# An attention and feed-forward block on one core: a re-ordered start, with the first pair's weight columns split first

## The chip, the core and the metric

The kernel runs on one core of a Trainium2 chip. A core has a matrix engine (TensorE, PE in the profile, with its weight loads shown as PEld), a vector engine (DVE), a scalar engine (ACT), a general engine (GpSimd, POOL) and a queue engine (SP) that starts most transfers. The engines run their own instruction streams in order and wait for one another through semaphores. The metric is the time of one execution on the device in microseconds (us).

## What is computed

The input x has 8 batches of 512 rows of 256 numbers. Cut to what matters, the reference is:

```python
x = x + attention(layernorm(x))    # rms_norm with gamma, w_qkv (256 x 3072), 16 heads of 64, softmax, w_out
x = x + ffn(layernorm(x))          # gelu(x @ w1 + b1) @ w2 + b2, scaled by the sum of the top-2 router weights
```

Everything is in 32-bit floating point. The first normalisation is a layernorm followed by an rms norm whose gamma is folded into w_qkv; attention is `softmax(q k^T / 8) v` for 8 x 16 heads.

## The kernel before, in words

**Arithmetic.** Every product is made from 16-bit operands in three parts. An operand is split into a high part (the value scaled and rounded to 16 bits, written by ACT) and a low part (what the rounding lost, written by DVE with a `SCALAR_TENSOR_TENSOR`, or on POOL for the softmax numerators). The three products are high x high, low x high and high x low (`PARTS`). The scale is a power of two, found on the chip from a sum of squares: `square` (ACT) squares a weight block and sums along the row, `total` adds over the 128 partitions with a product with ones on PE into the PSUM tile `pn`, and `powers` works out the exponent with seven tiny DVE instructions. `with_gamma` multiplies the factor by `gam1` = 1 + gamma, on DVE. `find_qk` does this for half of the q and k columns (512 each, four pairs of heads); its second part `rest()` (seven more tiny DVE instructions) finds the output scale `ab` that the eviction of q and k needs. `find_v` does it for v.

**The start.** `load_x(0)`, gamma and the blocks q0, k0, v0, v1 of w_qkv are loaded at once, into the four buffers of the pool `stage`; q1 and k1 (columns 512 to 1023) and the inputs of batches 1 to 3 stand behind them on SP, and q1 and k1 wait for buffers of `stage`. PE meanwhile runs `WARM` = 80 products of zeros into a bank of the pool `ps_m`. DVE finds mean and variance of batch 0 (`sums1`), `scale1` turns them into factors (two POOL instructions with the operation pow), `normalize` writes the normalised rows, and `transpose_rows` turns them with PE into the tile `pt` and splits them into `xnT`. `part_qk` splits the q0 and k0 blocks 512 columns at a time into `wqk`, and `project_qk(0, n)` makes q and k of the first pair of heads; its `high` is an ACT instruction into `QT` or `KT`, its `low` a DVE instruction.

**The loop.** The attention part has 128 steps. A step takes two tiles of scores: `scores` on PE into the two double buffers of `ps_s`, `top` (the row maximum, DVE, tile `mx`), `exp` (four ACT instructions into `e`), `high` (ACT casts e into `hl`), `low` (four POOL subtractions) and a transposing transfer on SP into `hT` (7 buffers). Three steps later `weigh` multiplies by V and `divide` (DVE) divides. A pair of heads of one batch has four tiles of scores, so it takes two steps. Everything else is hung on the steps by hand: `at(step, pos, fn, ...)` puts a piece of work at a place of a step. Within a step the order of issue is: the scores and their maxima, the low parts left over, `"d"`, the products of `"a"`, the exponentials, `"e"`, the evictions of `"a"` (high parts on ACT, then low parts on DVE), the casts of e, `weigh` and `divide`, `"b"`, `"z"`. `at` adds one to the step of every `"d"`. `Core.keep_order` keeps this order on all engines. So ACT and DVE, on which maxima, exponentials and all high and low parts lie, serve a step's items strictly in the written order.

In the first steps hang `split_wv` (w_v), `make_v` (V of batch 0), `project_qk` of the next pairs, the squares of q1 and k1 (`squares("qk1", ...)`, ACT, step 2), `find_qk` for them (step 3), `split_qk1` (steps 4 and 5), and for batch 1 `sums1` (step 1), `scale1` (steps 1 to 3), `normalize` (POOL, steps 3 and 4) and `transpose_rows` (steps 6 and 8).

After the attention steps comes the feed-forward part (`expand`, `contract`), which the change does not touch.

Of the kernel before, what the change touches and what calls it, by code (L numbers as in the profile page):

```python
# [11 lines left out]
F32 = mybir.dt.float32  # L12
F32R = mybir.dt.float32r
F16 = mybir.dt.float16
BF16 = mybir.dt.bfloat16
# [11 lines left out]
P = 128  # L27
LAG = 6
RING = 2
VW = 130  # L30
WARM = 80
EARLY = 6
# [44 lines left out]
def preln_block(  # L77
# [61 lines left out]
    for name, off, eng in (  # L139
        ("q0", 0, nc.scalar), ("k0", INNER, nc.sync), ("v0", 2 * INNER, nc.sync),  # L140
        ("v1", 2 * INNER + 512, nc.sync), ("q1", 512, nc.sync), ("k1", INNER + 512, nc.sync),
    ):
        raw[name] = staged(f"w_{name}", wqkv_r[:, :, off : off + 512], eng)
    for b in range(1, XB):
        load_x(b)
    w_r = const.tile([P, NC, NE], F32, name="w_r")
# [23 lines left out]

    def split(hi, lo, src, f):

        nc.scalar.activation(hi, src, AF.Copy, scale=f)
        return lambda: nc.vector.scalar_tensor_tensor(lo, src, f, hi, ALU.mult, ALU.subtract)
# [4 lines left out]
    def square(name, col, src, scale=1.0):  # L179

        pool, what = (hl_p, "hT") if name in ("qk0", "v") else (stage, "stage")
        junk = pool.tile([P, 1024], BF16, tag=what, name="junk", bufs=HTB if what == "hT" else SB)
        nc.scalar.activation(
            junk[:, 0 : src.shape[-1]], src, AF.Square, scale=scale,
            accum_out=sums[name][:, col[0], col[1] : col[1] + 1],
        )

    def square_v(name, col, src):
        junk = stage.tile([P, 512], BF16, tag="stage", name="junk")
        nc.vector.scalar_tensor_tensor(  # L190
            junk, src, 1.0, src, ALU.mult, ALU.mult,
            accum_out=sums[name][:, col[0], col[1] : col[1] + 1],
        )
# [41 lines left out]

    def with_gamma(name, s):

        f = stat.tile([P, 2, NC], F32, name=f"f_{name}")
        for i in range(2):
            nc.vector.tensor_scalar(f[:, i, :], gam1, s[:, i : i + 1], None, ALU.mult)  # L240
        return f

    def find_qk(half, n2):

        v = nc.vector
        added(n2)
        s, u, z = powers(f"qk{half}", n2)
        factors["qk", half] = with_gamma(f"qk{half}", s)  # L250

        def rest():
            ab = stat.tile([P, 2], U32, name=f"ab_{half}")
            w = stat.tile([P, 1], U32, name=f"w_{half}")
            v.tensor_copy(w, u[:, 1:2])
            v.tensor_tensor(z[:, 0:1], u[:, 0:1], w, ALU.add)
            v.tensor_scalar(z[:, 0:1], z[:, 0:1], 101, 254, ALU.add, ALU.min)
            v.tensor_scalar(w, z[:, 0:1], 1, None, ALU.logical_shift_right)
            v.tensor_tensor(u[:, 0:1], z[:, 0:1], w, ALU.subtract)
            v.tensor_scalar(ab[:, 0:1], u[:, 0:1], 23, None, ALU.logical_shift_left)  # L260
            v.tensor_scalar(ab[:, 1:2], w, 23, None, ALU.logical_shift_left)
            factors["out", half] = ab.bitcast(F32)

        return rest

    def find_v(n2):
        added(n2)
        s, u, z = powers("v", n2)
        factors["v"] = with_gamma("v", s)
        factors["1/v"] = inverses("v", u, z)  # L270
# [29 lines left out]
    with ExitStack() as att:  # L300
# [13 lines left out]
        VT = [work.tile([P, HEADS, VW], F16, tag=f"VT{r}", name=f"VT{r}") for r in range(NT)]  # L314

        wv = [work.tile([P, NC, INNER], F16, name=f"wv{i}") for i in range(2)]
        wo = [work.tile([P, NP, D], F16, name=f"wo{i}") for i in range(2)]
# [11 lines left out]

        def part_qk(n, half, c):  # L330
            i = "qk".index(n)
            hi, lo = (w[:, c, i, ts(half, 512)] for w in wqk)
            return split(hi, lo, raw[f"{n}{half}"][:, c], factors["qk", half][:, i, c : c + 1])

        def squares(name, i, key):
            for c in range(NC):
                square(name, (i, c), raw[key][:, c, :], gam1[:, c : c + 1])

# [9 lines left out]
        def split_qk1(n, c):  # L348
            part_qk(n, 1, c)()
            done("wqk")  # L350

        def split_wv(c, j):
            cols = ts(j, 512)
            f = factors["v"][:, j, c : c + 1]
            split(wv[0][:, c, cols], wv[1][:, c, cols], raw[f"v{j}"][:, c, :], f)()
            done("wv", j)
# [36 lines left out]

        def scale1(b, part):


            g = nc.vector if b == 0 else nc.gpsimd
            mv = norm1[b][0]
            if part == 0:
                rstd = tiny.tile([P, NT], F32, tag="rstd", name="rstd")  # L400
                g.tensor_scalar(rstd, mv[:, :, 1], LN_EPS, None, ALU.add)
                nc.gpsimd.tensor_tensor(rstd, rstd, halves[:, 0, :], ALU.pow)
                nm = tiny.tile([P, NT], F32, tag="nm1", name="nm1")
                g.tensor_scalar(nm, mv[:, :, 0], -1.0, None, ALU.mult)
                norm1[b] += [nm, rstd]
                return
            norm = tiny.tile([P, NT], F32, tag="norm", name="norm")
            g.tensor_scalar(norm, mv[:, :, 1], float(D), 1e-30, ALU.mult, ALU.max)
            nc.gpsimd.tensor_tensor(norm, norm, halves[:, 1, :], ALU.pow)
            _, nm, rstd = norm1[b]  # L410
            g.tensor_tensor(norm, norm, rstd, ALU.mult)
            g.tensor_scalar(norm, norm, NORM_EPS, float(D) ** -0.5, ALU.max, ALU.mult)
            norm1[b] = [nm, None, norm, rstd]
# [11 lines left out]
        def normalize(norm, b, t, tag):  # L425
# [5 lines left out]
            c = slice(t, t + 1)  # L431
            eng = nc.vector if (tag, b) == ("x", 0) else nc.gpsimd
            src = (xs if tag == "x" else x2)[b]
# [4 lines left out]
        def transpose_rows(b, c):  # L438

            if c == 0:  # L440
                xnT[b] = work.tile([P, NC, 2, S], F16, tag="xnT", bufs=2, name=f"xnT{b}")
            pt = bank("pt")
            need(NT, "xn", "x", b)
# [58 lines left out]
        def project_qk(pair, n):  # L502

            b, p = divmod(pair, NP)
            need(NC, "xnT", b)
            if p >= NP // 2:
                need(2 * NC, "wqk")
            pm = bank("pqk")
# [220 lines left out]

        warm = bank("warm")  # L730
        for i in range(WARM):
            nc.tensor.matmul(warm[:, 0:256], cold[:, 0:P], cold, start=True, stop=True)

# [5 lines left out]
        nc.vector.tensor_scalar_add(gam1, gam, 1.0)  # L739
        scale1(0, 0)  # L740
        scale1(0, 1)
        for name, k, m in (("qk0", 2, NC), ("v", 2, NC), ("qk1", 2, NC), ("o", 3, 1), ("w", 3, 4)):
            new_sums(name, k, m)
        for i in range(2):
            squares("qk0", i, "qk"[i] + "0")
        scale1_rest(0)
        scale1_last(0)
        for t in range(NT):
            normalize(norm1, 0, t, "x")
        squares("v", 0, "v0")  # L750
        rest = find_qk(0, total("qk0"))
        parts = [transpose_rows(0, c) for c in range(NC)]
        lows = [part_qk("q", 0, c) for c in range(NC)]
        for high, _ in parts:
            high()
        lows += [part_qk("k", 0, c) for c in range(NC)]
        for _, low in parts:
            low()
        for low in lows:
            low()  # L760
        rest()
        squares("v", 1, "v1")
        for high, low in [project_qk(0, n) for n in range(2)]:
            high()
            low()
        lows = [find(find_v, "v")[1]]


# [42 lines left out]

        for c in range(NC):
            at(0, "e", split_wv, c, 0)
            at(1, "e", split_wv, c, 1)
            at(4, "e", split_qk1, "q", c)
            at(5, "e", split_qk1, "k", c)
        for i in range(2):
            at(1, "d", squares, "qk1", i, "qk"[i] + "1")
        at(3, "b", find_rest, find_qk, 1, "qk1")
# [20 lines left out]
        for b in range(B):  # L840
# [10 lines left out]
            if b + 1 < B:  # L851
                at(max(s0 - 5, 1), "d", scale1_rest, b + 1)
                at(s0 - 4 if b else 2, "d", scale1_last, b + 1)
                for t in range(NT):
                    at(s0 + 21 + 2 * t, "a", project, b, 1, t)
                    at(max(s0 - 9 + t // 2, 0), "d", sums1, b + 1, t)
                    at(s0 + (1 + t if b else 2 + t // 2), "d", normalize, norm1, b + 1, t, "x")
                at(max(s0 - 7, 0), "d", scale1, b + 1, 0)
                at(max(s0 - 6, 0), "d", scale1, b + 1, 1)
                if b + XB < B:  # L860
                    for t in range(NT):
                        at(s0 + 30 + 2 * t, "d", load_x_piece, b + XB, t)
                for c in range(NC):
                    at(s0 + 6 + 2 * c, "b", transpose_rows, b + 1, c)
        del units[-2, "a"]
# [210 lines left out]
```

## Time and profile before

| what | us |
|---|---|
| median of 3 runs (971.69 to 971.80) | 971.78 |
| the profiled execution, its own time | 971.25 |
| its span, first to last instruction | 969.4 |
| PE busy in the span | 940.3 (97%) |
| ACT busy | 844.3 (87%) |
| DVE busy | 729.3 (75%) |
| POOL busy | 692.8 (71%) |
| mean granted TensorE clock | 0.996 |

A busy share is the time in which an engine's recorded instructions run. The granted clock is the share of full speed at which TensorE was let run. In the listings a row reads: start, length, engine, line (nearly always L48, the helper through which all instructions are issued, so tiles are what tells rows apart), operation, output tile, input tiles, shape, count, and in brackets how long the engine had stood idle and what released it.

### The profile page before, as it was taken

The numbers are of one execution on the slowest core, as the hardware profiler recorded it, in microseconds if no ns is written. First come the engines' busy times: TensorE is split into PE (matmuls) and PEld (weight loads), VectorE is DVE, ScalarE is ACT, GpSimd is POOL, SyncE is SP. The second block draws the span as 40 slices with busy tenths as digits, with TensorE's granted clock in tenths as the row PEclk, the third lists the DMA queues.
The fourth block names the chain that finished last, engine by engine and source line by source line (L and its number), as shares of the span: only waits on it lengthen the run. The fifth ranks groups of instructions, "written<-read, shape, count | busy, mean of one in ns | idle before, by whom it ended". The sixth has DMA issues, their size and how long they took to land.

```text
span 969.4 us, 27965 instructions
## 1 busy us (share of the span) xinstructions
PE 940.3 (97%) x11290; PEld 603.3 (62%) x11290; DVE 729.3 (75%) x1314; ACT 844.3 (87%) x1267; POOL 692.8 (71%) x713
## 2 busy tenths in 40 slices
PE   7788999999999999999999999999999999999998
PEld 5345566666666666666666666666666666666666
DVE  5878878988788878888877887777877865665554
ACT  5989899999999999999999999899999986767772
POOL 1677879788888888888888787877798963543400
PEclk9999999999999999999999999999999999999999
DMA  5598889999999999999989989889899991233111
GB/s 165 140 203 170 161 194 202 228 201 195 201 197 198 202 205 200 201 202 214 186 191 192 197 166 194 185 177 175 179 187 187 204 163 31 73 71 88 49 45 39
DMA packets 570193, 161.36 MB, mean 166 GB/s; under 512 B 552528, under 2 KB 568016, under 8 KB 570064
## 3 DMA queue, kind: packets, MB, share of 16 engines
q1 hardware_dynamic: 569520, 158.78, 80.3%
q8 instruction: 89, 1.46, 0.6%
q10 hardware_dynamic: 544, 0.79, 0.2%
q14 instruction: 40, 0.33, 0.1%
HBM read 14.82 MB, written 6.29 MB: 22 GB/s over the span
## 4 chain that ended last, share of the span: by engine, by line
PE 59%; DVE 18%; ACT 16%; issue 4%; POOL 2%; ACTq 0%; POOLq 0%
ACT e L48 11%; PE po L48 10%; PE ps L48 10%; PE pqk L48 9%; PE pf L48 9%; PE ph L48 8%; DVE mx L48 7%; PE pp L48 6%; PE pv L48 4%; DVE QT L48 2%; DVE KT L48 2%; DVE O L48 2%; DVE VT L48 2%; PE pot L48 2%; ACT QT L48 2%
## 5 line engine op out<-in xcount | busy, mean ns | idle before, releaser
L48 POOL TENSOR_TENSOR hl<-e,hl 128x512 f16<-128x512 f32 x512 | 583.5, 1171 | 139.8 <-issue 88.3
L48 ACT ACTIVATE e<-ps,mx 128x512 f32<-128x512 f32 x512 | 310.2, 690 | 52.2 <-DVE mx L48 44.6
L48 DVE TENSOR_REDUCE mx<-ps 128x2 f32<-128x1024 f32 x256 | 300.3, 1213 | 5.1 <-PE ps L48 5.0
L48 ACT CAST hl<-e 128x1024 f16<-128x1024 f32 x256 | 259.2, 1083 | 0.0
L48 PEld LDWEIGHTS <-hT 128*128 128x128 f16 x6144 | 203.5, 97 | 32.3 <-issue 4.4
L48 PE MATMUL po<-VT,hT 128*128 128x65 f16 (+1 forms) x6144 | 207.9, 193 | 1.4 <-DVE VT L48 0.8
L48 PE MATMUL ps<-KT,QT 64*128 64x512 f16 x1536 | 192.1, 380 | 11.8 <-ACT e L48 10.4
L48 PE MATMUL pqk<-xnT,wqk 128*128 128x512 f16 x768 | 178.8, 382 | 7.6 <-DVE VT L48 3.7
L48 PEld LDWEIGHTS <-wqk 128*128 128x128 f16 x768 | 70.3, 98 | 111.8 <-issue 33.2
L48 PEld LDWEIGHTS <-QT 64*128 64x128 f16 x1536 | 67.3, 94 | 90.4 <-issue 28.1
L48 DVE SCALAR_TENSOR_TENSOR QT<-pqk,ab,QT 128x512 f16<-128x512 f32 x64 | 48.0, 750 | 77.6 <-ACT QT L48 77.6
L48 DVE SCALAR_TENSOR_TENSOR h<-h,s_w,h 128x512 f16<-128x512 f32 x64 | 50.1, 784 | 62.9 <-ACT h L48 62.9
L48 PE MATMUL pp<-wo,OT 128*128 128x256 f16 x768 | 95.1, 273 | 0.1
L48 PE MATMUL pv<-wv,xnT 128*128 128x512 f16 x384 | 93.3, 379 | 1.8 <-DVE QT L48 1.6
L48 PEld LDWEIGHTS <-OT 128*128 128x128 f16 x768 | 70.2, 98 | 33.0 <-issue 11.8
L48 PE MATMUL ph<-yT,w1s 128*128 128x512 f16 x384 | 89.6, 379 | 0.1
L48 PE MATMUL pf<-w2s,h 128*128 128x256 f16 x768 | 88.4, 273 | 0.0
L48 ACT ACTIVATE h<-ph,b,si_w 128x512 f32<-128x512 f32 x64 | 49.3, 770 | 41.7 <-PE ph L48 41.5
L48 PEld LDWEIGHTS <-h 128*128 128x128 f16 x768 | 75.1, 98 | 14.5
L48 DVE TENSOR_TENSOR VT<-pv,VT 128x512 f16<-128x512 f32 x64 | 43.8, 689 | 52.5 <-ACT VT L48 52.5
L48 PEld LDWEIGHTS <-xnT 128*128 128x128 f16 x384 | 37.3, 98 | 37.0 <-issue 4.9
L48 PEld LDWEIGHTS <-w1s 128*128 128x128 f16 x384 | 37.0, 98 | 36.8 <-issue 0.3
(128 smaller groups left out, 856.4 us busy)
## 6 DMA issues: line engine op xcount, KB each, us to landing
hT<-hl SPq DMA_TRANSPOSE x256, 3.9
w<-in_L_ffn_w_dram SPq DMA_DIRECT2D x32, 128.0 KB, 2.7
out_dram<-res SPq DMA_DIRECT2D x32, 128.0 KB, 1.7
x<-x SPq DMA_DIRECT2D x16, 128.0 KB, 2.6
x<-in_L_attn_x_dram SPq DMA_DIRECT2D x16, 128.0 KB, 2.8
x2s<-x SPq DMA_DIRECT2D x4, 512.0 KB, 3.6
x<-in_L_attn_x_dram SPq DMA_DIRECT2D x3, 512.0 KB, 8.1
w_k<-in_L_attn_w_qkv_dram SPq DMA_DIRECT2D x2, 512.0 KB, 6.2
```

Source lines behind the costliest of these rows:

```text
L48: i = method(*args, **kw)
```

## The change

- The squares of v0 and of k1 move from ACT to DVE (`square_v` with the factor `gam2` = gam1 squared); those of q1 are issued earlier, before the loop and in step 0; those of k1 at the ends of steps 1 and 2.
- q0 and k0 are split in three pieces of columns: the first 128 (the first pair of heads), the next 128, and the last 256. The low parts of the first piece come before the rest; `rest()` stands between the low parts of q and those of k; the last piece's low parts and `find_v` come in step 0.
- `with_gamma` becomes two tiny ACT instructions.
- `scale1` uses one pow instruction on 8 columns in place of two on 4. Of batch 0's four `normalize` instructions two move to POOL.
- `WARM` becomes 54 products at the start, 12 after the first transposes and 8 after the first pair's projections. The warming products and the first transposes use the two buffers of `ps_s`, no longer banks of `ps_m`.
- q1 and k1 are loaded by four transfers into buffers of the tag `OT`, which are free at the start, so they and the inputs of batches 1 to 3 wait for nothing.
- `split_wv` of the second half moves from step 1 to steps 2 and 3; for batch 1 `sums1` moves to steps 2 and 3, `scale1` to step 4, `normalize` to steps 6 and 7, `transpose_rows` to steps 8 and 9.

```diff
 VW = 130
-WARM = 80
+WARM = 54, 12, 8
 EARLY = 6
...
         ("q0", 0, nc.scalar), ("k0", INNER, nc.sync), ("v0", 2 * INNER, nc.sync),
-        ("v1", 2 * INNER + 512, nc.sync), ("q1", 512, nc.sync), ("k1", INNER + 512, nc.sync),
+        ("v1", 2 * INNER + 512, nc.sync),
     ):
-        raw[name] = staged(f"w_{name}", wqkv_r[:, :, off : off + 512], eng)
-    for b in range(1, XB):
-        load_x(b)
+        t = staged(f"w_{name}", wqkv_r[:, :, off : off + 512], eng)
+        raw[name] = [t[:, c, :] for c in range(NC)]
     w_r = const.tile([P, NC, NE], F32, name="w_r")
...
-    def split(hi, lo, src, f):
-
-        nc.scalar.activation(hi, src, AF.Copy, scale=f)
+    def split(hi, lo, src, f, eng=nc.scalar):
+
+        if eng is nc.scalar:
+            eng.activation(hi, src, AF.Copy, scale=f)
+        else:
+            eng.tensor_scalar(hi, src, f, None, ALU.mult)
         return lambda: nc.vector.scalar_tensor_tensor(lo, src, f, hi, ALU.mult, ALU.subtract)
...
-        pool, what = (hl_p, "hT") if name in ("qk0", "v") else (stage, "stage")
+        pool, what = (hl_p, "hT") if name in ("qk0", "v", "qk1") else (stage, "stage")
         junk = pool.tile([P, 1024], BF16, tag=what, name="junk", bufs=HTB if what == "hT" else SB)
...
-    def square_v(name, col, src):
-        junk = stage.tile([P, 512], BF16, tag="stage", name="junk")
+    def square_v(name, col, src, scale=1.0):
+        pool, what, n = (hl_p, "hT", HTB) if name in ("v", "qk1") else (stage, "stage", SB)
+        junk = pool.tile([P, 512], BF16, tag=what, name="junk", bufs=n)
         nc.vector.scalar_tensor_tensor(
-            junk, src, 1.0, src, ALU.mult, ALU.mult,
+            junk, src, scale, src, ALU.mult, ALU.mult,
             accum_out=sums[name][:, col[0], col[1] : col[1] + 1],
...
-    def with_gamma(name, s):
-
-        f = stat.tile([P, 2, NC], F32, name=f"f_{name}")
+    powers_of = {}
+
+    def with_gamma(*key):
+
+        f = stat.tile([P, 2, NC], F32, name="f_" + "".join(map(str, key)))
+        s = powers_of[key if len(key) > 1 else key[0]]
+        factors[key if len(key) > 1 else key[0]] = f
         for i in range(2):
-            nc.vector.tensor_scalar(f[:, i, :], gam1, s[:, i : i + 1], None, ALU.mult)
-        return f
+            nc.scalar.activation(f[:, i, :], gam1, AF.Copy, scale=s[:, i : i + 1])
...
         s, u, z = powers(f"qk{half}", n2)
-        factors["qk", half] = with_gamma(f"qk{half}", s)
+        powers_of["qk", half] = s
...
         s, u, z = powers("v", n2)
-        factors["v"] = with_gamma("v", s)
+        powers_of["v"] = s
         factors["1/v"] = inverses("v", u, z)
...
+        for name, off in (("q1", 512), ("k1", INNER + 512)):
+            raw[name] = []
+            for c in range(NC):
+                t = work.tile([P, 512], F32, tag="OT", name=f"w_{name}", bufs=8)
+                nc.sync.dma_start(out=t, in_=wqkv_r[:, c, off : off + 512])
+                raw[name].append(t)
+        for b in range(1, XB):
+            load_x(b)
+
         wv = [work.tile([P, NC, INNER], F16, name=f"wv{i}") for i in range(2)]
...
-        def part_qk(n, half, c):
+        def part_qk(n, half, c, cols=slice(0, 512), eng=nc.scalar):
             i = "qk".index(n)
-            hi, lo = (w[:, c, i, ts(half, 512)] for w in wqk)
-            return split(hi, lo, raw[f"{n}{half}"][:, c], factors["qk", half][:, i, c : c + 1])
-
-        def squares(name, i, key):
-            for c in range(NC):
-                square(name, (i, c), raw[key][:, c, :], gam1[:, c : c + 1])
+            hi, lo = (w[:, c, i, ts(half, 512)][:, cols] for w in wqk)
+            src = raw[f"{n}{half}"][c][:, cols]
+            for p in range(cols.start // P, cols.stop // P):
+                done("wqk", NP // 2 * half + p)
+            return split(hi, lo, src, factors["qk", half][:, i, c : c + 1], eng)
+
+        def squares(name, i, key, chunks=range(NC)):
+            for c in chunks:
+                square(name, (i, c), raw[key][c], gam1[:, c : c + 1])
...
             part_qk(n, 1, c)()
-            done("wqk")
...
             f = factors["v"][:, j, c : c + 1]
-            split(wv[0][:, c, cols], wv[1][:, c, cols], raw[f"v{j}"][:, c, :], f)()
+            split(wv[0][:, c, cols], wv[1][:, c, cols], raw[f"v{j}"][c], f)()
             done("wv", j)
...
-        def scale1(b, part):
+        def scale1(b):
...
             mv = norm1[b][0]
-            if part == 0:
-                rstd = tiny.tile([P, NT], F32, tag="rstd", name="rstd")
-                g.tensor_scalar(rstd, mv[:, :, 1], LN_EPS, None, ALU.add)
-                nc.gpsimd.tensor_tensor(rstd, rstd, halves[:, 0, :], ALU.pow)
-                nm = tiny.tile([P, NT], F32, tag="nm1", name="nm1")
-                g.tensor_scalar(nm, mv[:, :, 0], -1.0, None, ALU.mult)
-                norm1[b] += [nm, rstd]
-                return
-            norm = tiny.tile([P, NT], F32, tag="norm", name="norm")
-            g.tensor_scalar(norm, mv[:, :, 1], float(D), 1e-30, ALU.mult, ALU.max)
-            nc.gpsimd.tensor_tensor(norm, norm, halves[:, 1, :], ALU.pow)
-            _, nm, rstd = norm1[b]
+            both_p = tiny.tile([P, 2, NT], F32, tag="norm", name="norm")
+            g.tensor_scalar(both_p[:, 0, :], mv[:, :, 1], LN_EPS, None, ALU.add)
+            g.tensor_scalar(both_p[:, 1, :], mv[:, :, 1], float(D), 1e-30, ALU.mult, ALU.max)
+            nc.gpsimd.tensor_tensor(both_p, both_p, halves, ALU.pow)
+            nm = tiny.tile([P, NT], F32, tag="nm1", name="nm1")
+            g.tensor_scalar(nm, mv[:, :, 0], -1.0, None, ALU.mult)
+            rstd, norm = both_p[:, 0, :], both_p[:, 1, :]
             g.tensor_tensor(norm, norm, rstd, ALU.mult)
...
             c = slice(t, t + 1)
-            eng = nc.vector if (tag, b) == ("x", 0) else nc.gpsimd
+            eng = nc.vector if (tag, b) == ("x", 0) and t >= NT // 2 else nc.gpsimd
             src = (xs if tag == "x" else x2)[b]
...
                 xnT[b] = work.tile([P, NC, 2, S], F16, tag="xnT", bufs=2, name=f"xnT{b}")
-            pt = bank("pt")
+            pt = bank("pt") if b else first_s[:, c, :]
             need(NT, "xn", "x", b)
...
             need(NC, "xnT", b)
-            if p >= NP // 2:
-                need(2 * NC, "wqk")
+            need(2 * NC, "wqk", p)
             pm = bank("pqk")
...
-        warm = bank("warm")
-        for i in range(WARM):
-            nc.tensor.matmul(warm[:, 0:256], cold[:, 0:P], cold, start=True, stop=True)
+        warm = ps_s.tile([P, 2, S], F32, tag="ps", name="warm")
+        first_s = ps_s.tile([P, 2, S], F32, tag="ps", name="first_s")
+
+        def warm_up(n):
+            for i in range(n):
+                nc.tensor.matmul(warm[:, 0, 0:256], cold[:, 0:P], cold, start=True, stop=True)
+
+        warm_up(WARM[0])
...
         nc.vector.tensor_scalar_add(gam1, gam, 1.0)
-        scale1(0, 0)
-        scale1(0, 1)
+        gam2 = stat.tile([P, NC], F32, name="gam2")
+        scale1(0)
         for name, k, m in (("qk0", 2, NC), ("v", 2, NC), ("qk1", 2, NC), ("o", 3, 1), ("w", 3, 4)):
...
             squares("qk0", i, "qk"[i] + "0")
+        nc.vector.tensor_tensor(gam2, gam1, gam1, ALU.mult)
         scale1_rest(0)
...
             normalize(norm1, 0, t, "x")
-        squares("v", 0, "v0")
         rest = find_qk(0, total("qk0"))
+        with_gamma("qk", 0)
+        for c in range(NC):
+            square_v("v", (0, c), raw["v0"][c], gam2[:, c : c + 1])
         parts = [transpose_rows(0, c) for c in range(NC)]
-        lows = [part_qk("q", 0, c) for c in range(NC)]
+        warm_up(WARM[1])
         for high, _ in parts:
             high()
-        lows += [part_qk("k", 0, c) for c in range(NC)]
+        cols = slice(0, P)
         for _, low in parts:
             low()
-        for low in lows:
+        wq, wk = [[part_qk(n, 0, c, cols) for c in range(NC)] for n in "qk"]
+        cols = slice(P, 2 * P)
+        next_lows = [part_qk(n, 0, c, cols) for n in "qk" for c in range(NC)]
+        for low in wq:
             low()
         rest()
-        squares("v", 1, "v1")
-        for high, low in [project_qk(0, n) for n in range(2)]:
+        for low in wk:
+            low()
+        pairs = [project_qk(0, n) for n in range(2)]
+        warm_up(WARM[2])
+        for high, low in pairs:
             high()
             low()
-        lows = [find(find_v, "v")[1]]
+        squares("v", 1, "v1")
+        squares("qk1", 0, "q1", [0])
+        for low in next_lows:
+            low()
+        cols = slice(2 * P, 4 * P)
+        last_lows = [part_qk(n, 0, c, cols) for n in "qk" for c in range(NC)]
+        lows = []
+
+        def start_v():
+            find_v(total("v"))
+
+        def take_last():
+            for low in last_lows:
+                low()
...
         for c in range(NC):
+            if c == 0:
+                at(0, "e", with_gamma, "v")
+                at(4, "e", with_gamma, "qk", 1)
             at(0, "e", split_wv, c, 0)
-            at(1, "e", split_wv, c, 1)
+            at(2 + c, "e", split_wv, c, 1)
             at(4, "e", split_qk1, "q", c)
             at(5, "e", split_qk1, "k", c)
-        for i in range(2):
-            at(1, "d", squares, "qk1", i, "qk"[i] + "1")
+        at(-1, "d", start_v)
+        at(-1, "d", take_last)
+        at(-1, "d", squares, "qk1", 0, "q1", [1])
+        for c in range(NC):
+            at(1 + c, "b", square_v, "qk1", (1, c), raw["k1"][c], gam2[:, c : c + 1])
         at(3, "b", find_rest, find_qk, 1, "qk1")
...
             if b + 1 < B:
-                at(max(s0 - 5, 1), "d", scale1_rest, b + 1)
-                at(s0 - 4 if b else 2, "d", scale1_last, b + 1)
+                at(s0 - 5 if b else 4, "d", scale1_rest, b + 1)
+                at(s0 - 4 if b else 4, "d", scale1_last, b + 1)
                 for t in range(NT):
                     at(s0 + 21 + 2 * t, "a", project, b, 1, t)
-                    at(max(s0 - 9 + t // 2, 0), "d", sums1, b + 1, t)
-                    at(s0 + (1 + t if b else 2 + t // 2), "d", normalize, norm1, b + 1, t, "x")
-                at(max(s0 - 7, 0), "d", scale1, b + 1, 0)
-                at(max(s0 - 6, 0), "d", scale1, b + 1, 1)
+                    at(s0 - 9 + t // 2 if b else 1 + t // 2, "d", sums1, b + 1, t)
+                    at(s0 + (1 + t if b else 5 + t // 2), "d", normalize, norm1, b + 1, t, "x")
+                at(s0 - 6 if b else 3, "d", scale1, b + 1)
                 if b + XB < B:
...
                 for c in range(NC):
-                    at(s0 + 6 + 2 * c, "b", transpose_rows, b + 1, c)
+                    at(s0 + (6 + 2 * c if b else 8 + c), "b", transpose_rows, b + 1, c)
         del units[-2, "a"]
```

## The prediction

> **What bounds the kernel now.** I read first the busy time of each engine in stretches (PE, PEld, DVE, ACT, POOL; then clock, DMA share and GB/s):
>
> ```profile
> 10.00:20.00 10.00, 6.13 (x35) 3.44 (x33) 7.55 (x25) 6.71 (x16) 0.00 (x0) 0.88 0.09 22
> 60.00:80.00 20.00, 15.56 (x214) 9.49 (x213) 13.74 (x21) 18.70 (x32) 12.08 (x11) 1.00 0.90 187
> 150.00:200.00 50.00, 50.00 (x675) 32.05 (x673) 44.40 (x75) 46.58 (x72) 43.34 (x41) 1.00 1.11 215
> ```
>
> From 150 us on PE has work all the time; to about 110 us ACT is the fullest engine. Nothing in the change makes PE's later work smaller, so it can gain only what it moves the start forward, and what arrives at 60 us arrives at the end. PE's timeline shows the start:
>
> ```profile
> 1.23 10.21 PE L48 MATMUL warm<-cold 128*128 128x256 f16 x80 [1.23 <-POOL cold L48]
> 11.27 0.28 PE L48 MATMUL pn<-sums_qk,ones 128*128 128x4 f32 x2
> 15.84 1.02 PE L48 MATMUL pqk<-xnT,wqk 128*128 128x512 f16 x4 [3.36 <-DVE xnT L48]
> 17.77 3.17 PE L48 MATMUL pqk<-xnT,wqk 128*128 128x512 f16 x7 [0.27 <-DVE wqk L48]
> ```
>
> The sum `pn` starts when the warming ends, not when its squares do. The first projection waits for a PSUM bank, and k's products end only at 20.94. ACT's timeline shows who waits next:
>
> ```profile
> 10.19 0.19 ACT L48 ACTIVATION_READ_ACCUMULATOR junk<-w_k,gam 128x1 f32 x1
> ...
> 20.97 0.69 ACT L48 ACTIVATE KT<-pqk,ab 128x512 f16<-128x512 f32 x1
> 24.19 2.42 ACT L48 ACTIVATE e<-ps,mx 128x512 f32<-128x512 f32 x4 [2.53 <-DVE mx L48]
> ...
> 31.52 2.42 ACT L48 ACTIVATE e<-ps,mx 128x512 f32<-128x512 f32 x4 [0.29 <-DVE mx L48]
> ...
> 38.35 0.77 ACT L48 ACTIVATE junk<-w_q,gam 128x512 bf16<-128x512 f32 x1
> ...
> 41.18 2.43 ACT L48 ACTIVATE e<-ps,mx 128x512 f32<-128x512 f32 x4
> ```
>
> The four rows into e mark steps; those of steps 0 to 5 start at 24.19, 31.52, 41.18, 47.45, 51.63 and 61.26. Step 2's stand 2.9 us behind the squares of q1 and k1. A step is a loop: maxima (1.2 to the first), exponentials (2.35 for the four), high parts (0.5 to 0.65 each), the last low part (0.7), the next maxima.
>
> **The sum, up to the first scores.** The last squares of k0 are read out at 10.38, so with 54 products (the trace has 51 of the 80 done by 8.27, the other 29 take 3.17, 0.11 each: 54 end near 8.6) `pn` starts at 10.45, 0.8 earlier; its reduction starts at 10.8 (11.59) and the exponent is ready at 12.2 (12.98). DVE's two `normalize` rows (0.41 each) and the tiny square of gamma must be out of its way by then: pow on 4 columns takes 1.03 and 1.01, so on 8 it lies between 1.0 and 2.0; I take 1.9, near the two together, as a plain product on 4 columns takes 0.20 and most of pow therefore goes with the columns. Normalising then starts at 9.95 as now (9.91), DVE's pair ends at 10.7, POOL's (0.55 each when free) at 11.1 to 12, and the transposes (1.07) at 12.2 to 13.0. If POOL and DVE hinder each other, up to 0.4 of this is on the path; I take 0.1.
>
> From 12.2 DVE sets the pace: two squares of v0 at 0.70 (two split rows take 1.41), `xnT`'s lows 1.3, q's lows, `rest` 1.2, k's lows. A piece of 128 columns has no row; the DVE split takes 0.29 on 16 columns and 0.74 on 512, so 0.40, and 0.31 in a stream where neighbours overlap by 0.09. Bounds are 0.20 and 0.66. ACT's rows (0.31 on 16, 0.71 on 512) give the same, and 0.42 for 256 columns. So 12.2 + 0.1 + 1.4 + 1.3 + 0.6 + 1.2 + 0.6 = 17.4, k's last product 0.4 later, its ACT high part ends at 18.5. Before, that was at 21.66: 3.2 us. ACT's own chain (two `with_gamma` at 0.2, two `xnT` highs 1.05, eight pieces 2.5) ends at 16.2 and hides behind DVE's. The eight warming products (0.9) stand between k's projection and the scores, and end with k's high part.
>
> **The same, through the steps.** Here ACT takes much of it back. Behind k's high part stand, before the first exponentials, v1's squares (two at 0.71), one of q1, four pieces (1.7) and the other of q1: 4.5 us, so they start at 23.0 (24.19): 1.2 gained. The maximum, behind k's low part and four low pieces, is ready at 21.7 and not late. Step 1: exponentials end 25.35, `with_gamma` 0.35, w_v's highs 1.25, Q and K highs 1.15, K's low part 0.9, maximum 1.2: 30.2, gain 1.3. Step 2: end 32.5, three V highs 1.6, the last low 0.9, one square of k1 0.75, maximum 1.2: 36.95, gain 4.2, as the four squares are out of ACT's way. Step 3: end 39.25, w_v high 0.65, Q, K and V highs 1.65, last low 1.1, k1's other square 0.75 to 1.4, maximum 1.2: 44.6 to 45.3, gain 2.8 to 2.1. Step 4: end 47.0 (or 0.65 later throughout), w_v high and low 1.35, `divide` 0.6, maximum 1.2: 50.15 to 50.8, gain 1.5 to 0.8. Batch 1's `sums1` (1.1 in each of two steps) hides beside the exponentials. Step 5, from the start of step 4's maxima at 48.95: DVE's two maxima and the finding with `rest` (2.35 and 2.55; without `with_gamma`, whose pair took 1.40 there), q1's lows 1.4, Q, K and `divide` 1.9, maximum 1.2: 58.3 to 59.0, gain 3.0 to 2.3. From here both kernels do the same work, with ACT full. I take 2.5, nearer to the end with POOL in the way.
>
> The risk in this is DVE beside POOL. The row of another square on DVE, later, is the one to go by (ns: least, median, most):
>
> ```profile
> L48 DVE SCALAR_TENSOR_TENSOR junk<-w x5: 814/1360/1416, 150.7 to 197.9; 128x512 bf16<-128x512 f32 x5
> ```
>
> The same form takes 0.74 in the splits, while POOL has nothing, and 1.36 to 1.42 here, beside its subtractions. v0's squares run while POOL has nothing, k1's (near 35 and 42.5) just as POOL's subtractions of a step begin. [...]
>
> The warming cut has its own price. Before, a pause of 3.36 us on PE (12.48 to 15.84) was followed by a granted clock of 0.50 from 17.7 to 21.0, and seven products took 3.17 where about 1.5 is usual. The new pauses are 8.6 to 10.45, 1.85 us, and what the 12 products (1.3 at 0.11) leave open between the transposes and q's first high at 14. Shorter than the pause that cost the clock, so I take no loss; the other bound is a half clock from 10.8 to 14.2, which stretches transposes and warming by up to 2.3 us, to about 16, and ends k's products 0.3 late. A faster clock than before at 17.7 is not counted as a gain, as DVE sets the pace there.
>
> The remaining edits cost nothing: transfers of q1, k1 and batches 1 to 3 move from 17.8 to 3.3 on SP, ahead of the first transposing transfer at 32.65, and behind v1 in their queue; k0 lands at 8.64, used at 8.87, and the copies asked for after it (v0, v1) land later. Batch 1's rows are normalised at steps 6 and 7 in place of 3 and 4, its transposes come at 8 and 9, and V of batch 1 needs them at 11; if POOL (12.08 busy of 20 at 60 to 80) fell a step behind, there would still be one.
>
> Before: 971.25 for the profiled execution (span 969.4 and 1.85 around it). After: 968.75, and the median lies 0.53 above that execution: 969.3. A measurement tells about 0.2%, 1.94 us, from no change.
>
> **Rivals.** *ACT and DVE give it back.* Pieces at 0.45 in place of 0.31 add 0.56 to DVE's chain (four) and 0.56 to ACT's queue before the exponentials (four), and POOL takes 0.65 from one square: 2.5 - 1.75 = 0.75 is left, 971.0. For it: DVE is 99% busy from 30 to 40 us in the profile. Against: POOL's subtractions start only as k1's squares do.
>
> *POOL's factors in one step (slower).* For batches 2 to 7 `scale1` now does in one step what it did in two: 0.24 + 0.25 and 0.8 to 1.0 of pow come on top in the step before DVE's reciprocal, and POOL's subtractions come some 1.35 later. The reciprocal starts 1.56, 1.85, 1.56, 1.55 and 2.0 us after POOL is ready in five batches, so it just holds. For it: ACT already waits once for POOL there (0.99 us at 190.78). If all 1.35 in six batches reached PE, 8.1 us would be lost: 977.4. It decides from 0.75 per batch (4.5 in all). Against: PE shows no idle time in these places, so waits on ACT are taken up by its buffers.
>
> *The change doesn't do what it says:* one pow is as long as two, and the pause brings the clock down. Both are in the sum; with pow, pause and the hindrance of POOL and DVE at their worst ends (0.1, 0.3, 0.3) it is 970.0, inside the forecast.
>
> **How the numbers follow.** Forecast 969.3, with its own range from 967.9 (gain 3.0, and eight pieces at 0.20 give 0.9 more) to 970.5 (gain 2.3 less 1.1 for pieces at 0.45): chance 0.63, of which 0.05 lie above 969.84. Give-back, 971.0: 0.23. POOL: 0.14. Hence faster 0.58, same 0.28, slower 0.14. The range reaches up to the give-back with k1's other square waiting too (0.65), 971.7, and down to 966.8, where step 2's lead of 4.2 is kept and pieces are at their bound.
>
> **What would show it.** `pn` at 10.4 to 10.6; first pieces of `wqk` at 0.40; K's high part ending at 18 to 19; exponentials at 23.0, 30.2, 37, 45, 50.5 and 58.6; k1's squares at 0.75 or 1.4; pow of 8 near 1.9. I am wrong if step 5's exponentials are not 2 us earlier, or if they are and the end isn't; then PE idles beside the later reciprocals.

## The result, and the profile after

The changed kernel takes 990.12 us (median of 6 runs, 987.73 to 991.32), the kernel before 972.25 in the same comparison: a ratio of 1.0180, 95% interval 1.0169 to 1.0191. It is 1.8% slower. 969.3 was predicted. Its profiled execution took 989.82 with a span of 987.9, 18.5 us longer than before (969.4).

The start is not where this comes from. PE's timeline of the changed kernel (start, length, engine, line, operation, output and inputs, shape, count, idle time ahead and its releaser):

```profile
1.23 8.05 PE L48 MATMUL warm<-cold 128*128 128x256 f16 x54 [1.23 <-POOL cold L48]
10.74 0.38 PE L48 MATMUL pn<-sums_qk,ones 128*128 128x4 f32 x2 [1.45 <-ACT junk L48]
...
14.36 3.57 PE L48 MATMUL pqk<-xnT,wqk 128*128 128x512 f16 x12 [0.98 <-ACT wqk L48]
```

And ACT's timeline of it, with the rows that mark k's high part and steps 0 to 5:

```profile
17.97 0.69 ACT L48 ACTIVATE KT<-pqk,ab 128x512 f16<-128x512 f32 x1 [0.29 <-PE pqk L48]
...
22.97 2.39 ACT L48 ACTIVATE e<-ps,mx 128x512 f32<-128x512 f32 x4
...
30.28 2.46 ACT L48 ACTIVATE e<-ps,mx 128x512 f32<-128x512 f32 x4 [0.29 <-DVE mx L48]
...
37.03 2.42 ACT L48 ACTIVATE e<-ps,mx 128x512 f32<-128x512 f32 x4 [0.95 <-DVE mx L48]
...
44.67 2.42 ACT L48 ACTIVATE e<-ps,mx 128x512 f32<-128x512 f32 x4 [1.08 <-DVE mx L48]
...
50.26 2.42 ACT L48 ACTIVATE e<-ps,mx 128x512 f32<-128x512 f32 x4 [0.68 <-DVE mx L48]
...
58.25 2.42 ACT L48 ACTIVATE e<-ps,mx 128x512 f32<-128x512 f32 x4 [0.90 <-DVE mx L48]
```

The squares are out of ACT's way in step 2, and step 5's exponentials start at 58.25 in place of 61.26, 3.0 us earlier. In step 12 (103.14 against 105.83) 2.7 of it is still there. So 21 us are lost after that. The page of the changed kernel says to what (the queue that carries the transposing transfers, the chain that ended last, the costliest groups with the idle time ahead of them, and the transfers' time from issue to landing):

```profile
q1 hardware_dynamic: 569552, 158.78, 92.9%
...
PE 27%; ACT 25%; DVE 19%; DMA 16%; issue 7%; POOL 5%; ACTq 0%; POOLq 0%
...
L48 ACT CAST hl<-e 128x1024 f16<-128x1024 f32 x256 | 262.4, 1079 | 29.8 <-DMA hT<-hl 29.8
L48 PEld LDWEIGHTS <-hT 128*128 128x128 f16 x6144 | 205.7, 97 | 48.4 <-DMA hT<-hl 17.0
L48 PE MATMUL po<-VT,hT 128*128 128x65 f16 (+1 forms) x6144 | 212.6, 193 | 15.1 <-DMA hT<-hl 13.1
...
hT<-hl SPq DMA_TRANSPOSE x256, 4.9
```

The same lines of the kernel before:

```profile
q1 hardware_dynamic: 569520, 158.78, 80.3%
...
PE 59%; DVE 18%; ACT 16%; issue 4%; POOL 2%; ACTq 0%; POOLq 0%
...
L48 ACT CAST hl<-e 128x1024 f16<-128x1024 f32 x256 | 259.2, 1083 | 0.0
L48 PEld LDWEIGHTS <-hT 128*128 128x128 f16 x6144 | 203.5, 97 | 32.3 <-issue 4.4
L48 PE MATMUL po<-VT,hT 128*128 128x65 f16 (+1 forms) x6144 | 207.9, 193 | 1.4 <-DVE VT L48 0.8
...
hT<-hl SPq DMA_TRANSPOSE x256, 3.9
```

The queue moves the same 158.78 MB, but takes 92.9% of the DMA engines' time in place of 80.3%, of a longer span. The 256 transfers from `hl` to `hT` land 4.9 us after issue in place of 3.9. ACT waits 29.8 us for them (a new `hl` needs a buffer that a transfer still reads), PE for `hT`. None of these waits stands in the profile of before.

Where the time goes is read from stretches (each engine's busy time and instruction records, then granted clock, DMA share and GB/s). Before:

```profile
100.00:200.00 100.00, 96.96 (x1259) 61.01 (x1257) 83.94 (x142) 92.06 (x141) 82.40 (x79) 1.00 0.99 194
200.00:300.00 100.00, 100.00 (x1319) 63.20 (x1315) 81.84 (x132) 93.78 (x143) 85.52 (x85) 1.00 1.01 201
300.00:400.00 100.00, 99.08 (x1318) 63.24 (x1318) 82.96 (x139) 93.84 (x142) 84.11 (x81) 1.00 1.00 201
400.00:500.00 100.00, 100.00 (x1322) 62.65 (x1316) 81.92 (x127) 95.43 (x145) 84.00 (x81) 1.00 1.02 200
500.00:600.00 100.00, 100.00 (x1325) 63.52 (x1324) 77.22 (x123) 92.30 (x139) 82.88 (x81) 1.00 0.93 184
```

After:

```profile
100.00:200.00 100.00, 98.14 (x1260) 61.23 (x1257) 85.05 (x135) 91.49 (x137) 80.79 (x77) 1.00 1.05 184
200.00:300.00 100.00, 95.58 (x1251) 60.00 (x1249) 77.13 (x123) 87.75 (x135) 79.38 (x79) 1.00 1.13 190
300.00:400.00 100.00, 95.08 (x1234) 59.60 (x1231) 77.50 (x132) 87.91 (x133) 77.15 (x72) 1.00 1.14 188
400.00:500.00 100.00, 96.51 (x1245) 60.27 (x1244) 79.07 (x121) 91.61 (x138) 80.74 (x79) 1.00 1.11 190
500.00:600.00 100.00, 99.66 (x1318) 63.19 (x1317) 76.05 (x123) 91.46 (x137) 82.57 (x81) 1.00 1.16 191
```

From 200 to 500 us PE gets through 68, 84 and 77 products fewer than before: 229, at 13.2 a microsecond 17.3 us. The DMA share there was already 1.00 to 1.02 in the kernel before (it can exceed 1, as the packets' times are added up), and is 1.11 to 1.14 now at fewer GB/s. So the transfers had no room, and became the bound of this stage.

A high share alone is no proof of that. From 500 us on the changed kernel's share is as high (1.15 and 1.16 up to 700 us), and PE loses nothing: there the kernel before moves only 184 GB/s, and the slower transfers still reach 185 to 191. From 200 to 500 us it moved 200 to 201, and the changed kernel reaches 188 to 190. The steps say the same. Against the change with its tiles put back (e1 below), the maxima of step 28 start at the same time (198 us, within 0.1), those of step 80 19.6 us later (523 against 503), and those of step 124 18.6 later. Some 2 us more come after the attention steps; their cause stays open.

**Why the transfers are slower.** The trace has a record of every packet; the transposing transfers make 540,672 packets of 256 bytes. Before, 98% of them take 18 ns or less, mean 20.9; after, 82%, mean 25.0. Bytes and packets are the same; what differs is where the tiles lie. By the compiled program's addresses, which no profile here holds, tiles are laid out one after the other in each partition, in the order of the pools; the experiments put this to the test (64 bytes put back in e1, and 96 in e8, bring the landing back to 3.9 and 4.0 us). The change removes the tile `rstd` from the pool `tiny` (three buffers of 32 bytes) and adds `gam2` (32 bytes) to `stat`: all pools behind them, `hl_p` among them, move by -96 + 32 = -64 bytes. Each `hl` tile began on a multiple of 512 bytes; now it begins 448 bytes past one. `hT` moves in the same way.

### The profile page after: what moved, and what is told of

Read it like the earlier page. It is cut to its first block, busy times and chain, and to the rows that moved or that the text cites. A ratio compares the mean times of both kernels' runs of the same rounds, so it can differ in the third digit from the quotient of the medians.

```text
span 987.9 us, 27957 instructions
## 1 busy us (share of the span) xinstructions
PE 948.9 (96%) x11284; PEld 605.5 (61%) x11284; DVE 731.2 (74%) x1323; ACT 845.4 (86%) x1273; POOL 690.2 (70%) x707
## 3 DMA queue, kind: packets, MB, share of 16 engines
q1 hardware_dynamic: 569552, 158.78, 92.9%
## 4 chain that ended last, share of the span: by engine, by line
PE 27%; ACT 25%; DVE 19%; DMA 16%; issue 7%; POOL 5%; ACTq 0%; POOLq 0%
DMA hT<-hl 15%; ACT e L48 15%; PE pf L48 8%; DVE mx L48 8%; PE ph L48 7%; POOL hl L48 4%; ACT hl L48 4%; PE pqk L48 3%; PE po L48 3%; DVE QT L48 2%; PE ps L48 2%; DVE O L48 2%; DVE KT L48 2%; DVE VT L48 2%; ACT QT L48 2%
## 5 line engine op out<-in xcount | busy, mean ns | idle before, releaser
L48 ACT CAST hl<-e 128x1024 f16<-128x1024 f32 x256 | 262.4, 1079 | 29.8 <-DMA hT<-hl 29.8
L48 PEld LDWEIGHTS <-hT 128*128 128x128 f16 x6144 | 205.7, 97 | 48.4 <-DMA hT<-hl 17.0
L48 PE MATMUL po<-VT,hT 128*128 128x65 f16 (+1 forms) x6144 | 212.6, 193 | 15.1 <-DMA hT<-hl 13.1
L48 PE MATMUL ps<-KT,QT 64*128 64x512 f16 x1536 | 194.8, 380 | 8.9 <-ACT e L48 7.3
```

The source lines that it names most:

```text
L48: i = method(*args, **kw)
```

## The experiments

Theory: the 64 bytes, and the transfer's reads of `hl` above all, cost the 20 us, and the change's own work gains what was forecast. Rivals: the transfer's writes to `hT`; POOL's factors in one step; the new order of loads and splits. All kernels compute the whole reference.

### The change, with the tiles put back: e1_after_plus64

```diff
-        gam2 = stat.tile([P, NC], F32, name="gam2")
+        gam2 = stat.tile([P, NC + 16], F32, name="gam2")[:, 0:NC]
```

> The changed kernel, with the tile gam2 made 64 bytes per partition longer and nothing else; that puts hl, hT and all tiles behind the small ones back on the byte offsets of the kernel before (hl and hT at a multiple of 512 bytes; the change moved them to 448 past one). Theory 1 (the place in memory): the transposing transfers land in 3.9 us as before, their 256-byte packets take 18 ns, and the time is 968.7, from 967.5 to 970, 3 us under the kernel before. Theory 2 (the new order itself, for example factors on POOL in one step, or other collisions of transfers): transfers stay at 4.9 us and the time at 988 to 991. Theory 3 (the loads put into OT buffers, which moved the tiles of the pool work against each other): as theory 2.

Measured: 968.81 us against 972.63 for the kernel before, ratio 0.9962 (0.9947 to 0.9977). Landing 3.9 us, queue 81.2%, PE at 100 to 99 of each 100 us between 200 and 500 again; its span is 966.9, 2.5 below before. 64 unused bytes are worth 21 us.

### The kernel before, with the tiles moved: e2_before_plus448

```diff
-    comb = stat.tile([P, B, NT], F32, name="comb")
+    comb = stat.tile([P, B * NT + 112], F32, name="comb")[:, 0 : B * NT]
+    comb = comb.rearrange("p (b t) -> p b t", t=NT)
```

> The kernel before, with the tile comb 448 bytes per partition longer and nothing else, so that hl and hT stand 448 bytes past a multiple of 512 as in the changed kernel. Theory 1: the transfers land in 4.9 us, the time rises to 988 to 994. Theories 2 and 3: 972, transfers 3.9 us.

Measured: 992.57 us, ratio 1.0215 (1.0198 to 1.0232), landing 5.0, mean packet 24.9 ns. The same instructions, 448 bytes further on, lose what the change loses. The two together give the change: 1.0215 times e1's 0.9962 is 1.0176, and 1.0180 was measured.

### Writes or reads: e3_before_hT64 and e4_before_hl64

Two unused tiles in `hl_p` (a memset of each at the start) move one of the two tags alone by 64 bytes. For `hT`, `pa` stands ahead of it and `pb` (448 bytes) between it and `hl`; for `hl`, `pa` stands between them:

```diff
+        pa = hl_p.tile([P, 16], F32, tag="pa", name="pa", bufs=1)
+        nc.gpsimd.memset(pa, 0.0)
```

> The kernel before, with the seven hT buffers (which the transposing transfers write) moved to 64 bytes past a multiple of 512, and hl and all else left on their offsets (two small tiles are put in around hT). Theory 1a (writes that do not start on a boundary cost more): transfers near 4.9 us, time 985 to 994. Theory 1b (reads do): 972 and 3.9 us. Theories 2 and 3: 972.

> The kernel before, with the five hl buffers (which the transposing transfers read) moved to 64 bytes past a multiple of 512, hT and all else left on their offsets. Theory 1a (writes): 972 and 3.9 us. Theory 1b (reads): transfers near 4.9 us, time 985 to 994. Theories 2 and 3: 972.

Measured, `hT` moved: 972.16, ratio 0.9996 (0.9987 to 1.0005), landing 4.0. `hl` moved: 993.72, ratio 1.0216 (1.0200 to 1.0231). The latter's page has:

```profile
hT<-hl SPq DMA_TRANSPOSE x256, 5.0
```

So it is the reads. Moving the place where the transfer writes by 64 bytes makes no difference that can be measured.

### Which boundary: e5_before_hl128 and e6_before_hl256

As e4, with spacers of 128 and 256 bytes.

> The kernel before, with two idle spacers in the pool of hl, so that every hl tile begins 128 bytes past a multiple of 512 in its partition, and hT stays where it was. Theory (the transposing transfer reads its 256-byte pieces fast only from a 256-byte boundary): slow as with 64 bytes, 990 to 994 us, hT landing after 4.9 to 5.0 us. Rival (a boundary of 64 or 128 bytes is enough): 972 us and 3.9 us.

> The kernel before, with two idle spacers in the pool of hl, so that every hl tile begins 256 bytes past a multiple of 512. Theory (a 256-byte boundary decides): as before, 972 us, hT landing after 3.9 us. Rival (a 512-byte boundary decides, as hl's rows are 2048 bytes apart): slow, 990 us or more, about 5 us.

Measured: 128 bytes 992.05 (ratio 1.0203, 1.0186 to 1.0220), landing 4.9; 256 bytes 972.44 (1.0001, 0.9992 to 1.0011). The page with 256 bytes:

```profile
hT<-hl SPq DMA_TRANSPOSE x256, 3.9
```

The boundary is 256 bytes, the size of a packet. All runs by the place of `hl`:

| `hl`, bytes past a multiple of 512 | kernels | mean packet, ns | landing, us | against before |
|---|---|---|---|---|
| 0 | before, e1, e3, e8, e9 to e12 | 20.9 to 21.5 | 3.9 to 4.0 | 0 (e3, e8); with the change -0.3% to -0.5% (e1, e9 to e12) |
| 256 | e6 | 21.0 | 3.9 | 0 |
| 64 | e4 | 24.7 | 5.0 | +2.2% |
| 128 | e5 | 24.7 | 4.9 | +2.0% |
| 416 | e7 | 24.9 | 5.1 | +2.2% |
| 448 | after, e2 | 25.0, 24.9 | 4.9, 5.0 | +1.8%, +2.2% |

Off the boundary the place counts for little: the mean packet is 24.7 ns at 64 and 128 bytes and 24.9 to 25.0 at 416 and 448. What happens inside the DMA engine no run here shows.

### One part of the change alone: e7_before_pow1 and e8_before_pow1_plus96

```diff
-        def scale1(b, part):
+        def scale1(b):
...
-                rstd = tiny.tile([P, NT], F32, tag="rstd", name="rstd")
...
+            both_p = tiny.tile([P, 2, NT], F32, tag="norm", name="norm")
...
+            nc.gpsimd.tensor_tensor(both_p, both_p, halves, ALU.pow)
```

In e8, `comb` is also 96 bytes longer.

> The kernel before with one part of the change alone: scale1 in one call with one pow of 8 columns, for all batches. The tiny tile rstd goes, and with it hl moves to 416 bytes past a multiple of 512. Theory (place in memory alone): 990 to 994 us, hT landing about 5 us, though the work is all but the same. Rival (POOL's factors in one step): 975 to 980 us, hT landing 3.9 us, DVE waiting for POOL before its reciprocals.

> The same as the kernel with scale1 in one call, and comb made 96 bytes longer, so that hl is back on a multiple of 512. Theory (place alone): 971.5 to 973 us, 3.9 us. Rival (POOL's factors in one step): 975 to 980 us, as the place has nothing to do with it.

Measured: e7 992.94 (1.0218, 1.0203 to 1.0234), e8 972.09 (1.0001, 0.9991 to 1.0010). The one pow instruction costs 2.2% through the 32-byte tag that it no longer needs, and nothing through its work. In e8, as in before, POOL's `low` waits 16.6 us in all for the group of factors, and DVE waits for POOL only in batch 0. That settles the rival "POOL's factors in one step".

### What the start is worth: e9, e10, e11, e12

All four are the changed kernel with `gam2` longer by 64 bytes (e1's edit), with one more edit.

e9_after64_warm80:

```diff
-WARM = 54, 12, 8
+WARM = 80, 12, 8
```

> The changed kernel with gam2 made 64 bytes longer (hl back on a multiple of 512), and 80 warming products at the start in place of 54. By the sum: pn at 11.3 in place of 10.45, everything to the first scores up to 0.8 later, of which ACT's queue takes up part; first exponentials 23.2 to 23.9, the end 0.2 to 0.8 later than with 54: 969.0 to 969.6 us. Rival (the clock gains from the longer warming): granted clock from 14 to 18 us higher, and the end no later than 968.8.

Measured: 970.11, against 972.59 for before (0.9972, 0.9961 to 0.9983); `pn` at 11.35, first exponentials 23.48 (23.06 in e1), and every later step 0.42 to 0.44 behind e1's, span 0.6 longer. The clock was 1.00 from 5 to 25 us, and still the end is no earlier: the rival falls. The median is 0.5 above the range expected; the intervals of the two ratios (e1: 0.9947 to 0.9977) overlap.

e11_after64_nowarm2:

```diff
-WARM = 54, 12, 8
+WARM = 54, 0, 0
```

> The changed kernel with gam2 made 64 bytes longer, and without the 12 warming products behind the first transposes and the 8 behind the first projections (54, 0, 0). By the sum: nothing on the path changes but the clock; if the pauses on PE (up to 2 us before q's products) cost no clock, exponentials within 0.2 of those with the products (23.0, 30.3) and 968.8 us. Rival (a pause of over 3 us brings the granted clock to half, as in the kernel before): k's products end 1 to 2 us later, exponentials at 23.5 to 24.5, and the end up to 1.5 later, 970.

Measured: 969.98 (0.9971, 0.9959 to 0.9982); exponentials at 24.22 and 31.53, 1.2 behind e1's. Stretches of it:

```profile
12.00:14.00 2.00, 1.25 (x6) 0.85 (x4) 1.65 (x6) 1.19 (x4) 0.00 (x0) 0.50 1.07 388
14.00:16.00 2.00, 1.28 (x4) 0.51 (x5) 1.60 (x4) 2.00 (x7) 0.00 (x0) 0.50 1.10 362
16.00:18.00 2.00, 2.00 (x6) 0.73 (x5) 1.68 (x10) 1.20 (x4) 0.00 (x0) 0.50 0.48 152
```

and of e1, which has the 20 small warming products:

```profile
12.00:14.00 2.00, 2.00 (x11) 1.63 (x10) 1.67 (x6) 1.46 (x5) 0.00 (x0) 0.50 1.07 388
14.00:16.00 2.00, 2.00 (x14) 1.10 (x11) 1.88 (x5) 2.00 (x8) 0.00 (x0) 0.89 1.10 363
16.00:18.00 2.00, 1.88 (x10) 0.73 (x10) 1.59 (x10) 1.11 (x3) 0.00 (x0) 1.00 0.52 164
```

The granted clock is 0.50 in both from 12 us, after pauses on PE of 1.65 (e11) and 1.83 us (e1); with the small products it is back at 1.00 before q's and k's products, without them not before 18. So the rival's price was right: in these profiles the small products are worth 1.2 us (the medians, 969.98 and 968.81, differ by as much, but the intervals of the two ratios overlap). Its cause was not: the clock fell without a pause of over 3 us, in both, and what the products do is to bring it back sooner.

e10_after64_actsq puts k1's two squares back on ACT, both in step 2:

```diff
-            at(1 + c, "b", square_v, "qk1", (1, c), raw["k1"][c], gam2[:, c : c + 1])
+            at(1, "d", squares, "qk1", 1, "k1", [c])
```

> The changed kernel with gam2 made 64 bytes longer, and the two squares of k1 back on ACT, both in step 2. By the sum: ACT has 1.4 to 1.6 more between step 1's and step 2's exponentials, DVE loses 0.75 in steps 2 and 3 each; step 2's exponentials 1.0 to 1.6 later (38.1 to 38.7), step 3's 0.5 to 1.0 later, step 5's 0 to 0.8 later, the end 0 to 0.8: 968.8 to 969.6 us. Rival (squares on DVE cost as much as they give): the same exponentials from step 3 on, 968.8.

Measured: 967.66 (0.9948, 0.9935 to 0.9962), below the range expected; neither step 2 nor step 3 is later. ACT's timeline of e10, steps 2, 3 and 5:

```profile
37.10 2.44 ACT L48 ACTIVATE e<-ps,mx 128x512 f32<-128x512 f32 x4
...
44.08 2.42 ACT L48 ACTIVATE e<-ps,mx 128x512 f32<-128x512 f32 x4 [0.41 <-DVE mx L48]
...
57.66 2.42 ACT L48 ACTIVATE e<-ps,mx 128x512 f32<-128x512 f32 x4 [0.90 <-DVE mx L48]
```

e1 has 37.12, 44.75 and 58.34. DVE, not ACT, ended e1's waits last (0.95 in step 2, 1.07 in step 3): a square on DVE stands ahead of the maxima, 0.67 each. On ACT the two squares fill the wait in step 2 and cost 0.3 of e10's lead there, and in step 3 no square stands ahead of the maxima. 0.35 of e10's lead of 0.68 in step 5 stands already at step 0 (22.71 against 23.06): 0.09 at `pn`, and the rest from e1's half clock after its pause of 1.83; e10's pause was 0.71. What is left, 0.33, is the squares', read from one profile of each; between the medians of e10 and e1 the intervals of the ratios overlap.

e12_warm66_actsq is e10 with 66 warming products:

```diff
-WARM = 54, 12, 8
+WARM = 66, 12, 8
```

> The changed kernel with gam2 made 64 bytes longer, k1's two squares on ACT in step 2, and 66 warming products at the start. By the rows: 66 products end at about 9.9 to 10.0, ahead of k0's squares (10.4), so pn is not delayed (10.5) and the pause on PE is 0.5 in place of 0.7 to 1.9 with 54, so that the half clock between 10.8 and 14.9, seen in one of the profiles with 54 products and worth 0.3, does not come. First exponentials 22.7, step 5's 57.7, span 965.7, median 967.4 to 967.8. Rival (the pause with 54 products costs nothing on the median, and 66 end too late): pn at 10.9 or later and 968.0 to 968.4.

Measured: 967.56 (0.9951, 0.9937 to 0.9965), as e10 and within the range expected, but not by the way expected. In its profiled run, the longest of its five (968.08), `pn` is at 11.17, as the 66 products ended only at 11.33. The first ones come at 7 a microsecond, and the switch to 12 came after 3 us in before and after 6 here. The profile prints a clock of 1.00 ahead of the switch too, but the trace's first record of the clock stands just there (at 3.92 us in before, at 6.84 here), so that figure is not measured. No count ends at a fixed time, then, and between 54 and 66 nothing is decided. e10 and e12 are the fastest versions: 0.5% below before, 2.3% below the change.

## Why the prediction was wrong, point by point

**The sum for the start was right.** `pn` was told for 10.45 and came at 10.74, 10.57 and 10.48 (after, e1, e10); K's high part ended at 18.66 (18.5 told); exponentials were told for 23.0, 30.2, 36.95, 44.6 to 45.3, 50.15 to 50.8 and 58.3 to 59.0, and came at 22.97, 30.28, 37.03, 44.67, 50.26 and 58.25. 2.5 us was taken to reach the end, and 2.5 did in e1 (spans 969.4 and 966.9). Between medians the gain of e1 was larger (3.8, of which the ratio's interval leaves 2.2 to 5.2). The median forecast, 969.3, lies 0.5 above what the change takes with its tiles put back (968.81).

**The step that failed** is "The remaining edits cost nothing", with "From here both kernels do the same work". The edits were costed as instructions and transfers. A tile that goes and one that comes were not costed as bytes, though the diff shows both: `rstd` out of `tiny`, `gam2` into `stat`, and two pools that come ahead of `hl_p`. From there on both kernels do the same instructions, but one of these, the transposing transfer, got slower. The price was 21 us, in a sum that came to a gain of 2.5. With it falls the sentence that what arrives at 60 us arrives at the end. The prediction's own sign of error came true (step 5 is 3.0 us earlier, the end is not), but PE does not idle beside the later reciprocals, as it said; PE and its weight loads wait for `hT` (13.1 and 17.0 us).

**A row that was shown hinted at it.** The row for 150 to 200 us, quoted to show that PE has work all the time, has a DMA share of 1.11 in the same line. In that very stretch the change lost nothing; the loss came from 200 us on, where the share before was 1.00 to 1.02. But had the transfers been read as a possible second bound, anything that could touch them would have needed a price.

**The rivals.** "POOL's factors in one step" had the sign (slower, 977.4) and a wrong mechanism; e8 shows that it costs nothing. "ACT and DVE give it back" did not come about: a piece of 128 columns took 0.40 by itself and 0.29 to 0.30 in a stream on ACT (0.40 and 0.31 taken). "Doesn't do what it says" neither: pow on 8 columns took 1.66 at the start (1.9 taken), against 1.03 and 1.01 for the two.

**DVE beside POOL** turned out with the roles changed. 1.4 was feared for k1's squares; they took 0.74. POOL's rows of e1, the four subtractions of each of steps 0 to 2:

```profile
29.21 4.50 POOL L48 TENSOR_TENSOR hl<-e,hl 128x512 f16<-128x512 f32 x4 [18.04 <-ACT hl L48]
35.30 4.95 POOL L48 TENSOR_TENSOR hl<-e,hl 128x512 f16<-128x512 f32 x4 [1.58 <-ACT hl L48]
42.80 5.06 POOL L48 TENSOR_TENSOR hl<-e,hl 128x512 f16<-128x512 f32 x4 [2.56 <-ACT hl L48]
```

The squares start at 35.14 and 42.77, just ahead, and POOL's fours take 4.95 and 5.06 in place of 4.50; in e10, without k1's squares on DVE, all three are 4.50. Here the second to start was POOL, and it paid 0.45 to 0.56. What decides which of the two pays no run here shows.

**The warming cut.** No loss of clock was taken for pauses under 3.36 us. Pauses of 0.71 (e10) and 1.45 (after) cost none; after 1.65 (e11) and 1.83 (e1) the clock was 0.50. The bound given for that, 0.3 us late, is what e1 shows against e10 (0.26). The length of a pause does not decide alone. In the traces of before, after and e1 the clock changes only at points that lie a multiple of 3.41 us apart, and where these points fall differs from run to run (the first at 3.92, 5.32 and 4.20 us). In e1 it changes at 4.20, 11.03 and 14.44: of the 3.41 us ahead of 11.03 PE idled 1.83, and from 11.03 to 14.44 the clock is 0.50. In before it changes at 3.92, 17.58 and 20.99, so that such a point at 14.16 splits the pause of 3.36: 1.68 idle in the 3.41 us ahead of it left the clock at 1.00, about 2.0 in the next (to 17.58) was followed by 0.50. A limit near half a stretch would fit these profiles (an estimate from the idle times just given: 1.68 below it, 1.83 and 2.0 above); no run tests it. 54 products were to end near 8.6; they ended between 8.73 and 9.77.

## What to carry to other kernels

A diff that adds or drops a small tile can move the tiles allocated behind it, here `hl` by 64 bytes for 21 us: work out the byte shift, and look which transfers read the tiles that move. Here the transposing transfers' packets of 256 bytes took 20.9 to 21.5 ns with the source tile on a 256-byte boundary and 24.7 to 25.0 off it: give the source of such a transfer a place on that boundary on purpose (a pad behind the small pools), and look for it first when a profile shows the same bytes at a higher DMA share (80.3% against 92.9% for this queue); other kinds of transfer were not tried here. And read the share of every resource in the stage that bounds the kernel, not only the engine that is never idle: a DMA share of 1.00 to 1.02 beside a busy PE stood here where slower transfers became the bound (200 to 500 us); at 0.91 to 0.93 (500 to 700 us) they did not, though the share rose to 1.15 and 1.16 there.

## What the runs showed of the hardware that was not expected

- Moving the source of the transposing transfers off a 256-byte boundary raised the mean packet from 20.9 ns to 24.7 to 25.0 and the landing from 3.9 us to 4.9 to 5.1, by nearly the same amount for 64, 128, 416 and 448 bytes; moving the destination by 64 bytes changed nothing (972.16 against 972.63).
- The 16 DMA engines' time in these packets grew by 138 us each (706.8 to 844.9), the kernel by 18.5: most of it was hidden, and the loss fell between 198 and 523 us, where the kernel before moves 200 to 201 GB/s at a share of 1.00 to 1.02.
- A pause of 1.65 us on PE was enough for a granted clock of 0.50, and 1.45 was not, in one profile each; in the traces of before, after and e1 the clock changed only at points a multiple of 3.41 us apart, so where a pause falls may count as well as its length.
